# Stores and expert-weight transfers of a fused attention and mixture-of-experts kernel, issued from other queues

## The chip, the cores and the metric

The kernel runs on 1 core of one Trainium2 chip. The metric is the device time of one execution in microseconds (us): the median of three runs. A separate execution is taken under the hardware profiler; every duration of a single instruction below comes from that one.

## What is computed

x is (2, 4096, 512), float32 throughout. For each of the two batches a condition vector gives six rows of shifts, scales and gates. Cut to what matters:

```
h   = layernorm(x) * (1 + ca) + sa
q, k, v = h @ w_qkv.T            # 16 heads of 32; q, k = relu(q), relu(k)
vk  = sum over all tokens of v (padded with ones) times k      # linear attention
x   = x + ga * ((vk @ q) / normaliser @ w_proj.T + b_proj)
h   = layernorm(x) * (1 + cb) + sb
logits = rmsnorm(h) @ router;  two of eight experts per token
x   = x + gb * sum over the two experts of weight * (gelu(h@Wg) * (h@Wv)) @ Wl
```

The sum over all tokens of a batch stands between two passes over that batch: the first makes q, k and the sum, the second needs the sum.

## The kernel before

**Tiling.** A block is 512 tokens of one batch, as four tiles of 128 partitions x 512 features; a batch has eight blocks. Large products go by a seven-product scheme (Strassen's, in Winograd's form) on quarters of the operands, so that both sides need precomputed sums of quarters.

**Stages.** *First passes* (`firsts`, `first`): for each block TensorE makes k and q in fourteen steps (line 717), VectorE scales them out of PSUM (728), ScalarE applies Relu in place (774), then TensorE multiplies x by k into the sum (`pa`, 795). The token-side sums of quarters are made by GpSimd in `turned_sums` (679 to 682): four operations on the transposed block xT that SyncE has loaded (201). In the first batch their target `xs` has one buffer, so line 679 of a block waits until TensorE has done the products of the block before; in TensorE's order the product that needs line 681 is the third of seven, that of 679 the fourth, that of 682 the last. *Second passes* (`seconds`): `attend` loads q tiles back (883), two tiles ahead, normalises, transposes and projects them, adds the residual (952) and stores x to `out` (974); `second_norm` makes h (994, 998; one buffer), stores it to `h_d` (1007), and `route` scatters token slots to `map_d` (1153). *Experts* (`block`, `smalls`): rows of h are gathered by expert, and TensorE runs gate and output products (1512, 1705, 1731); results are added to `out` by indirect transfers from GpSimd. The first pass of batch 1 runs among the second pass of batch 0, and the second pass of batch 1 among the first expert blocks.

**Expert weight sums.** The experts' products need sums of quarters of their weights too. `weight_sums` (584 to 621) makes them in 24 jobs during the first passes of batch 0: load 1 MB of weights into one of two buffers (`wraw`, 598), four GpSimd operations on 128x512 (617), store 1 MB back (618). Two loads are in flight ahead; the load for job n+2 stands behind the store of job n. The expert stage reads the sums after about 860 us. `firsts` takes one job at three points of every block (line 1233).

**What sets the order.** Each engine runs its own instruction stream in order, and a DMA is an instruction in the stream of the engine that issues it: if it has to wait, everything behind it waits. The order inside a stream is chosen at build time by a list scheduler from the order of the program's text and the steps of its generators. In the kernel before, all plain loads and the wraw stores are issued by SyncE (SP in the profile), the stores of q, `out` and h by ScalarE (ACT), and GpSimd (POOL) issues indirect transfers only. Plain transfers of SP and ACT share eight completion semaphores that are taken in turn, so that a transfer can also have to wait until the eighth one before it has landed; those of GpSimd have eight of their own.

Of the kernel before, what the change touches and what calls it, by code (L numbers as in the profile page):

```python
# [17 lines left out]
P = 128  # L18
B, N, C = 2, 4096, 512
# [7 lines left out]
NT = TB // P  # L27
NTOK = B * N
NBLK = N // TB
# [24 lines left out]
def adaln_linear_attention_moe_kernel(  # L54
# [27 lines left out]
    nc = tc.nc  # L82
# [17 lines left out]
        out=upper, in_=ones, compare_op=ALU.is_gt, fill=0.0, base=0,  # L100
# [69 lines left out]
    def place(n, tag, name):  # L170
        return psum["p"].tile([P, 512], FP, tag=f"{tag}{n}", name=name)
# [66 lines left out]
    raw = {}  # L238
# [345 lines left out]
    def weight_sums():  # L584


        jobs = []
        for e in range(E):
            rows = slice(e * P, (e + 1) * P)
            for m in range(2):  # L590
                src = wgate[rows, m * 4 * KH * QN : (m + 1) * 4 * KH * QN]
                r0 = (2 * e + m) * P
                jobs.append((src, wgsum_d[r0 : r0 + P, :], True))
            jobs.append((wlin[rows, :], wlsum_d[rows, :], False))

        def load(n):
            raw = temp(f"wraw_{n}")
            nc.sync.dma_start(out=raw.rearrange("p q n -> p (q n)"), in_=jobs[n][0])
            return raw

        ready = [load(0), load(1)]
        yield
        for n, (_, dst, left) in enumerate(jobs):
            raw = ready.pop(0)
            a, b, c, d = (raw[:, q, :] for q in range(4))
            if left:
                steps = (
                    (c, d, c, ALU.add), (d, a, d, ALU.subtract),
                    (a, c, a, ALU.subtract), (b, b, a, ALU.subtract),
                )  # L610
            else:
                steps = (
                    (a, d, a, ALU.subtract), (d, c, d, ALU.subtract),
                    (c, c, a, ALU.subtract), (b, b, c, ALU.subtract),
                )
            for to, one, two, op in steps:
                nc.gpsimd.tensor_tensor(to, one, two, op)  # L617
            nc.sync.dma_start(out=dst, in_=raw.rearrange("p q n -> p (q n)"))
            if n + 2 < len(jobs):
                ready.append(load(n + 2))  # L620
            yield


# [61 lines left out]
    def first(b, i, acc, ksum):  # L685

        xh, mv = prepared.pop((b, i))
        xs = turned.pop((b, i))
        ks, qs = {}, {}
        out_of = (ks, qs)  # L690
        tile0 = (b * NBLK + i) * NT
        alone = b == 0 and i == 0

        def banks_of(m, c):


            n = c if alone else m
            tags = ("one", "two") if alone or c == 0 else ("two", "one")
            return [place(n, tag, f"p{m}{tag}_{b}_{i}_{c}") for tag in tags]

        def lane(m, c):

            one, two = banks_of(m, c)
            at = E if m else 0
            top, low = slice(0, QN), slice(QN, C)
            for t in (c, c + 2):
                if m:
                    out_of[m][t] = row("qo", f"q_{b}_{i}_{t}", 4, ap)
                else:
                    out_of[m][t] = row("k", f"k_{b}_{i}_{t}", 4, ap)  # L710
            upper_t, lower_t = out_of[m][c], out_of[m][c + 2]

            def product(s, to):
                f = forms[m, s]
                a = at - (AHEAD.get(s, 0) if m else 0)
                for k in range(KH):
                    nc.tensor.matmul(
                        to[:, a : a + f.shape[2]], xs[s][:, k, c * P : (c + 1) * P],
                        f[:, k, :],
                        start=(k == 0 and s in (1, 2, 7)), stop=(k == KH - 1 and s in (2, 4, 3)),  # L720

                        skip_group_check=True,
                    )

            def keep(t, cols, src, new):

                to = out_of[m][t][:, cols]
                nc.vector.scalar_tensor_tensor(
                    to, src[:, at : at + QN], mv[:, t, 1:2],
                    bias[m, b][:, cols] if new else to, ALU.mult, ALU.add,  # L730
                )

            def logits(t, src, c0, new):
                to = xl[:, tile0 + t, 0:E]
                if new:
                    nc.vector.tensor_copy(to, src[:, c0 : c0 + E])
                else:
                    nc.vector.tensor_tensor(to, src[:, c0 : c0 + E], to, ALU.add)

            behind = at + QN  # L740
            for s in ORDER:
                to = two if s in (2, 7, 4) else one
                product(s, to)
                if s == 1:
                    keep(c, top, to, True)
                    if m:
                        logits(c, to, 0, True)
                elif s == 2:
                    keep(c, top, to, False)
                    if m:  # L750
                        logits(c, to, behind, False)
                elif s == 6:
                    keep(c + 2, top, to, True)
                elif s == 7:
                    keep(c + 2, low, to, True)
                elif s == 5:
                    keep(c + 2, low, to, False)
                    if m:
                        logits(c + 2, to, behind, True)
                elif s == 4:  # L760
                    keep(c + 2, top, to, False)
                    if m:
                        logits(c + 2, to, behind, False)
                else:
                    keep(c, low, to, True)
                yield
            for t in (c + 2, c):
                r = out_of[m][t]
                if m == 0:
                    if i == 0 and c == 0 and t == 2:  # L770
                        nc.vector.tensor_scalar(ksum, r, 0.0, None, ALU.max)
                    else:
                        nc.vector.scalar_tensor_tensor(ksum, r, 0.0, ksum, ALU.max, ALU.add)
                nc.scalar.activation(r, r, AF.Relu)  # L774
                if m:
                    r0 = (b * NBLK + i) * P
                    nc.scalar.dma_start(out=q_d[r0 : r0 + P, t * C : (t + 1) * C], in_=r)

        for lanes in (
            ((0, 0), (0, 1)), ((1, 0), (1, 1))  # L780
        ) if alone else (
            ((0, 0), (1, 0)), ((0, 1), (1, 1))
        ):
            going = [lane(*l) for l in lanes]
            for n, s in enumerate(ORDER):
                for g in going:
                    next(g)
                if n == len(ORDER) - 1:
                    for g in going:
                        next(g, None)  # L790
                yield
        for g in range(KC):
            pa = place(g // 2, ("one", "two")[g % 2], f"pa_{b}_{i}_{g}")
            for t in range(NT):
                nc.tensor.matmul(  # L795
                    pa, xh[t][:, g * P : (g + 1) * P], ks[t],
                    start=(t == 0), stop=(t == NT - 1),
                )
            if i == 0:
                nc.vector.tensor_copy(acc[:, g, :], pa)  # L800
            else:
                nc.vector.tensor_tensor(acc[:, g, :], pa, acc[:, g, :], ALU.add)
            yield
        if b + 1 < B and i == NBLK - 1:
            for n in range(2):
                spread_bias(n, b + 1)
# [89 lines left out]
    def attend(b, i, kall, gm):  # L896
# [3 lines left out]
        qs = {}  # L900
# [63 lines left out]
        for step in range(NT + 2):  # L964
            if step < NT:
                weigh(step)
            if 1 <= step <= NT:
                turn(step - 1)
            if step >= 2:
                project(step - 2)  # L970
            if step == NT and i + 1 < NBLK:
                load_xb(b, i + 1)
            if step == NT + 1:
                nc.scalar.dma_start(
                    out=out[r0 : r0 + TB, :].rearrange("(p t) c -> p t c", t=NT), in_=xt
                )
            yield

    def second_norm(b, i):
# [11 lines left out]
        for step in range(NT + 2):  # L991
            if step < NT:
# [10 lines left out]
                nc.scalar.activation(  # L1003
                    sq, h2[:, step, :], AF.Square, accum_out=ssq[:, j : j + 1]
                )
            if step == NT:
                nc.scalar.dma_start(
                    out=h2_d[r0 : r0 + TB, :].rearrange("(p t) c -> p t c", t=NT), in_=h2
                )
                if b + 1 < B and i == NBLK - 1:  # L1010
                    for n in (SB, CB):
                        batch_row(n, b + 1)
# [876 lines left out]
```

## Time and profile before

| what | value |
|---|---|
| median of 3 runs | 2304.97 us (2301.86 to 2310.61) |
| the profiled execution's own time | 2372.11 us |
| its span, first to last instruction | 2370.4 us |
| mean granted TensorE clock | 0.981 |
| HBM read, written | 378.97 MB, 132.55 MB |
| q0, transfers issued by GpSimd | 296.79 MB, 40.1% of the 16 DMA engines' span |
| q1, issued by SP | 164.45 MB, 20.4% |
| q10, issued by ACT | 50.34 MB, 5.5% |

The profiled execution takes 67 us (2.9%) more than the median of the runs. In its rows, L12 is a line of the kernel before; PE is TensorE's matmul, PEld its weight load, DVE is VectorE; a q behind an engine's name (SPq, ACTq) marks an issued DMA, which is not counted as busy time. `out<-in` names the tile written and the tile read; `[6.87 <-ACT k L774]` at the end of a row says that the engine was idle for 6.87 us before it, and what released it.

### The profile page before, as it was taken

How to read it: one execution, taken by the hardware profiler on the slowest of the kernel's cores; microseconds unless marked ns; L12 is line 12 of the kernel's file. 1: busy time of each engine (PE TensorE's matmuls, PEld its weight loads, DVE VectorE, ACT ScalarE, POOL GpSimd, SP SyncE). 2: the span in 40 equal slices, each digit the busy share in tenths (PEclk: the TensorE clock that was granted, in tenths of full speed). 3: DMA queues.
4: the chain of work that ended last, by engine and by line, in shares of the span. 5: the costliest groups of instructions: out<-in, count | busy, mean ns of one | idle time of the engine just before them, and what ended most of it. 6: DMA issues, size and time to landing. Idle time of an engine off the chain costs nothing. (4 is left out here: it accounts for less than half of the span.)

```text
span 2370.4 us, 26081 instructions
## 1 busy us (share of the span) xinstructions
PE 2257.7 (95%) x9456; PEld 1702.1 (72%) x9456; DVE 1523.0 (64%) x3251; ACT 535.0 (23%) x976; POOL 963.2 (41%) x840
## 2 busy tenths in 40 slices
PE   8999989999988999989998889999999999999997
PEld 4576657777766758878887767777777777777775
DVE  4866647786977756767876765555555555555554
ACT  1121212232323302333333411111111111111110
POOL 1266663003223242343535356444444444544432
PEclk9999999999999999999999989999999999999999
DMA  7688886444544444647684557777777777777774
GB/s 271 244 310 324 333 313 230 166 152 138 178 164 110 127 160 166 215 152 239 171 256 150 162 169 241 250 249 247 249 250 250 235 237 248 244 249 256 245 222 89
DMA packets 120189, 513.29 MB, mean 217 GB/s; under 512 B 19365, under 2 KB 22181, under 8 KB 84090
## 3 DMA queue, kind: packets, MB, share of 16 engines
q0 software_dynamic: 64704, 296.79, 40.1%
q1 hardware_dynamic: 41530, 164.45, 20.4%
q10 hardware_dynamic: 13824, 50.34, 5.5%
q8 instruction: 77, 1.26, 0.2%
q14 instruction: 54, 0.44, 0.1%
HBM read 378.97 MB, written 132.55 MB: 216 GB/s over the span
## 5 line engine op out<-in xcount | busy, mean ns | idle before, releaser
L1512 PE MATMUL p_g<-xT,wg 128*128 128x256 f32 x1600 | 373.0, 380 | 0.0
L1512 PEld LDWEIGHTS p_g<-xT,wg 128*128 128x128 f32 x1600 | 303.4, 191 | 45.7 <-issue 5.2
L1512 PE MATMUL p_g<-xS,wg 128*128 128x256 f32 x1200 | 286.6, 381 | 14.9 <-DVE quar_l L1520 7.6
L1512 PEld LDWEIGHTS p_g<-xS,wg 128*128 128x128 f32 x1200 | 227.4, 191 | 51.2 <-issue 8.1
L946 PE MATMUL po<-gm,qT 128*128 128x265 f32 (+1 forms) x1024 | 247.2, 391 | 4.6 <-issue 2.6
L795 PE MATMUL pa<-k,xh 128*128 128x512 f32 x512 | 234.2, 611 | 16.4 <-ACT k L774 16.3
L946 PEld LDWEIGHTS po<-gm,qT 128*128 128x128 f32 x1024 | 194.3, 194 | 40.2 <-issue 5.5
L1488 POOL DMA_INDIRECT out<-y_b,mp x100 | 162.7, 1627 | 129.2 <-DVE y_b L1485 101.2
L1153 POOL DMA_INDIRECT map_d<-pair,slot x128 | 133.5, 1043 | 176.0 <-DVE slot L1150 138.4
L1705 PE MATMUL pgs<-wgs,xTs 128*128 128x512 f32 x464 | 203.9, 592 | 0.0
L1512 PE MATMUL p_l<-wl,aT 128*128 128x256 f32 x800 | 193.7, 380 | 2.6 <-DVE part_l L1520 2.6
L795 PEld LDWEIGHTS pa<-k,xh 128*128 128x128 f32 x512 | 99.0, 196 | 134.4 <-issue 108.1
L617 POOL TENSOR_TENSOR wraw<-wraw 128x512 f32<-128x512 f32 x96 | 135.7, 1417 | 88.9 <-DMA wraw<-in_wgate 36.0
L1705 PEld LDWEIGHTS pgs<-wgs,xTs 128*128 128x128 f32 x464 | 88.2, 190 | 110.5 <-issue 109.5
L1512 PEld LDWEIGHTS p_l<-wl,aT 128*128 128x128 f32 x800 | 148.8, 191 | 23.6 <-DVE part_l L1520 3.0
L1512 PE MATMUL p_l<-wl,aS 128*128 128x256 f32 x600 | 144.0, 383 | 0.6 <-DVE aS L1622 0.6
L679 POOL TENSOR_TENSOR xs<-xT 128x512 f32<-128x512 f32 x16 | 21.3, 1330 | 292.1 <-DMA xT<-in_xturned 173.1
L1520 DVE TENSOR_TENSOR quar_g<-part_g,p_g 128x512 f32<-128x512 f32 x150 | 102.5, 684 | 51.1 <-PE p_g L1512 46.5
L1611 ACT ACTIVATE ge<-quar_g 128x512 f32<-128x512 f32 x100 | 63.0, 630 | 312.2 <-DVE quar_g L1520 300.9
L1512 PEld LDWEIGHTS p_l<-wl,aS 128*128 128x128 f32 x600 | 114.3, 192 | 17.9 <-issue 1.4
L1421 POOL DMA_INDIRECT xg_b<-h_d,mp x100 | 100.9, 1009 | 64.1 <-issue 32.5
L1520 DVE TENSOR_TENSOR part_g<-part_g,p_g 128x512 f32<-128x512 f32 x100 | 68.5, 686 | 83.8 <-PE p_g L1512 78.8
(343 smaller groups left out, 3734.7 us busy)
## 6 DMA issues: line engine op xcount, KB each, us to landing
xT<-in_xturned SPq DMA_DIRECT2D x16, 1024.0 KB
x<-in_x SPq DMA_DIRECT2D x16, 1024.0 KB
q_d<-q ACTq DMA_DIRECT2D x64, 256.0 KB
xb_d<-x SPq DMA_DIRECT2D x16, 1024.0 KB
qi<-q_d SPq DMA_DIRECT2D x64, 256.0 KB
wraw<-in_wgate SPq DMA_DIRECT2D x16, 1024.0 KB
wgsum_d<-wraw SPq DMA_DIRECT2D x16, 1024.0 KB
xb<-xb_d SPq DMA_DIRECT2D x16, 1024.0 KB
```

What stands on the lines that cost most here:

```text
L617: nc.gpsimd.tensor_tensor(to, one, two, op)
L679: nc.gpsimd.tensor_tensor(s7, x00, x10, ALU.subtract)
L795: nc.tensor.matmul(pa, xh[t][:, g * P : (g + 1) * P], ks[t], start=(t == 0), stop=(t == NT - 1),)
L946: nc.tensor.matmul(po[:, C // 2 - EX + c0 : C // 2 - EX + c1], qT[:, g * P : (g + 1) * P], gm[:, g, c0:c1], start=(g == 0), stop=(g == KC ...
L1153: ins = nc.gpsimd.indirect_dma_start(out=map_d, out_offset=IndirectOffsetOnAxis(ap=slot[:, k, t : t + 1], axis=0), in_=pair[:, k, t, :], i ...
L1421: return nc.gpsimd.indirect_dma_start(out=dst, out_offset=None, in_=src, in_offset=IndirectOffsetOnAxis(ap=ids, axis=0))
L1488: ins = nc.gpsimd.indirect_dma_start(out=out[0:N, :] if early else out, out_offset=IndirectOffsetOnAxis(ap=token(mp, t), axis=0), in_=y, i ...
L1512: nc.tensor.matmul(bank[:, c, :], left(s, c, k), rhs[:, k, :], start=(k == 0), stop=(k == KH - 1),)
L1520: nc.vector.tensor_tensor(r, one, two, ALU.add)
L1611: nc.scalar.activation(ge, g, AF.Gelu_apprx_tanh)
L1705: nc.tensor.matmul(p, xT[:, k, :], wg[:, :, quarters[k // KH], k % KH, :], start=(k == 0), stop=(k == KC - 1),)
```

## The change

The 64 stores of q tiles go from ScalarE's stream to SyncE's, and are written later in the text: the tiles of each lane pair together, ahead of the second and of the fourth `pa` product. The 16 stores of x to `out` and the 16 stores of h go from ScalarE's to SyncE's, those of h one generator step later. The 24 loads and 24 stores of the weight sums go from SyncE's to GpSimd's. One load is written ahead of the loop instead of two, and the load of job n+1 ahead of the four operations of job n.

```diff
@@ weight_sums
-            nc.sync.dma_start(out=raw.rearrange("p q n -> p (q n)"), in_=jobs[n][0])
+            nc.gpsimd.dma_start(out=raw.rearrange("p q n -> p (q n)"), in_=jobs[n][0])
             return raw
-        ready = [load(0), load(1)]
+        ready = [load(0)]
         yield
         for n, (_, dst, left) in enumerate(jobs):
+            if n + 1 < len(jobs):
+                ready.append(load(n + 1))
             raw = ready.pop(0)
...
             for to, one, two, op in steps:
                 nc.gpsimd.tensor_tensor(to, one, two, op)
-            nc.sync.dma_start(out=dst, in_=raw.rearrange("p q n -> p (q n)"))
-            if n + 2 < len(jobs):
-                ready.append(load(n + 2))
+            nc.gpsimd.dma_start(out=dst, in_=raw.rearrange("p q n -> p (q n)"))
             yield
@@ first, lane
                 nc.scalar.activation(r, r, AF.Relu)
-                if m:
-                    r0 = (b * NBLK + i) * P
-                    nc.scalar.dma_start(out=q_d[r0 : r0 + P, t * C : (t + 1) * C], in_=r)
@@ first
         for g in range(KC):
+            if g in (1, 3):
+                for t in range(g // 2, NT, 2):
+                    r0 = (b * NBLK + i) * P
+                    nc.sync.dma_start(
+                        out=q_d[r0 : r0 + P, t * C : (t + 1) * C], in_=qs[t]
+                    )
@@ attend
             if step == NT + 1:
-                nc.scalar.dma_start(
+                nc.sync.dma_start(
                     out=out[r0 : r0 + TB, :].rearrange("(p t) c -> p t c", t=NT), in_=xt
                 )
@@ second_norm
-            if step == NT:
-                nc.scalar.dma_start(
+            if step == NT + 1:
+                nc.sync.dma_start(
                     out=h2_d[r0 : r0 + TB, :].rearrange("(p t) c -> p t c", t=NT), in_=h2
                 )
```

In the built program of the changed kernel, GpSimd's stream in the first passes of batch 0 reads, from job 8 on, as a chain of: load of job n+1, store of job n, the four operations of job n+1, load of job n+2, and so on, with the four operations of `turned_sums` spread between them. For blocks 2 to 7 they stand within jobs 2 and 3, 7 and 8, 11 and 12, 15 and 16, 20, and behind job 21.

## The prediction

> **What bounds the kernel now.** I read the page's engine totals first, then the waits, then a table of the first-pass blocks of batch 0, then the timeline where TensorE stood still.
>
> ```profile
> PE 2257.7 (95%) x9456; PEld 1702.1 (72%) x9456; DVE 1523.0 (64%) x3251; ACT 535.0 (23%) x976; POOL 963.2 (41%) x840
> ```
>
> TensorE is busy 95% of the span: 112.7 us is all that any change of queues can give back, and whatever holds TensorE up is added in full. Waits, over the whole span and then from 100 to 400 us:
>
> ```profile
> PE pa L795 <- ACT k L774: 16.3, 4, 8.4
> ...
> POOL wraw L617 <- DMA wraw<-in_wgate: 36.0, 7, 6.8
> POOL wraw L617 <- DMA wraw<-in_wlin: 29.3, 6, 7.4
> ```
>
> Of all that ScalarE does, TensorE waits for Relu of k (16.3 us in 4 waits) and for little else. GpSimd waits 65 us for weights to land, and nobody waits for GpSimd: no row has TensorE behind it in these blocks. How near it is shows in the table by block (bounds from the first product of each) and the timeline.
>
> ```profile
> 265.40:306.30 40.90, 38.89 (x145) 27.11 (x144) 25.80 (x56) 7.93 (x13) 24.71 (x20) 1.00 0.88 335
> 306.30:355.40 49.10, 41.58 (x145) 28.28 (x144) 25.07 (x56) 8.05 (x13) 33.45 (x25) 0.90 0.84 319
> 355.40:395.90 40.50, 38.69 (x146) 27.21 (x145) 28.25 (x64) 8.04 (x13) 17.38 (x13) 1.00 0.79 291
> ```
>
> The columns are the stretch, PE, PEld, DVE, ACT, POOL, granted clock, DMA share, GB/s. A block takes 39.6 us, TensorE works 38.8 of it, GpSimd 25, the DMA engines 77 to 96% over the seven blocks of this table. The middle block took 49.1:
>
> ```profile
> 306.94 1.27 POOL L681 TENSOR_TENSOR xs<-xT 128x512 f32<-128x512 f32 x1
> ...
> 331.90 0.61 ACT L774 ACTIVATE q<-q 128x512 f32<-128x512 f32 x1
> 339.43 0.34 ACTq L777 DMA_DIRECT2D q_d<-q  x1
> 339.81 0.63 ACT L774 ACTIVATE k<-k 128x512 f32<-128x512 f32 x1 [7.29 <-DMA wlsum_d<-wraw]
> ...
> 340.49 7.80 PE L795 MATMUL pa<-k,xh 128*128 128x512 f32 x11 [6.87 <-ACT k L774]
> ```
>
> ScalarE stood at a store of q until a weight-sum transfer had landed; Relu of k stood behind it, TensorE behind that. After the gap 10.2 us ran at half clock (the 0.90 of this stretch: 4.9 us lost). And line 681 ended at 308.2 where TensorE needs it at 309.8 (block start 306.3 plus two products of 1.75): GpSimd had 1.6 us to spare.
>
> **Part 1, 96 stores leave ScalarE.** Their issue is not busy time and ScalarE is at 23%. What it frees is the wait above: 6.9 + 4.9 us, and about 1 us of smaller ones: -13 in this execution. On SyncE 96 x 0.33 us are added and 48 x 0.35 leave, beside a queue that mostly waits: nothing by itself. But SyncE's stream is passed in order: behind a q store that waits for Relu stand the loads of x and xT (needed a block, 40 us, later); behind an h store stands a load of q, needed by the next `attend` step. A step is (694.0 - 638.6) / 6 = 9.2 us. I take 0, with -3 and +30 as ends (the second rival).
>
> **Part 2, 48 transfers of 1 MB enter GpSimd's stream.** Three terms.
>
> Issue: no such transfer is in this trace. The nearest are the indirect loads of 128 rows from the same queue: 0.95 us each, so 46 us of GpSimd in all. Bounds are the 0.33 of SyncE's issues and the 1.6 of the indirect adds (L1488); as both issues of a job lie inside the wait for its load, neither moves the sum while L is over 2 x 1.6.
>
> Landing: for the same 1 MB from SyncE I find issue 276.24, operations released 282.51 (6.3); 358.64 to 363.64 (5.0, DMA share 0.79); most others 6.9 to 7.0. From GpSimd's queue there is
>
> ```profile
> 1405.09 0.30 issue
> 1405.39 3.81 DMA xg_b<-h_d,mp
> 1409.25 0.69 PE px L1579 x2
> ```
>
> 3.8 us for 256 KB; 768 KB more at 291 to 335 GB/s makes 6.2 to 6.5. I take L = 6.0, bounds 4.4 and 7. The lower end is the Trainium skill's (DMA: Bandwidth & Descriptors, "Anatomy of one DMA — SWDGE (gpsimd) path"), which fits a transfer from this queue as 2.0 us plus bytes over 436 GB/s: 4.4. The rows say longer, since other traffic keeps the DMA engines at over 0.79.
>
> Order: in the built program the load of job n+1 is issued right ahead of the operations that use it, in GpSimd's own stream. What was fetched ahead now is waited for: one job is L + 4 x 1.33 = 11.3 us (both issues lie inside L). Between the sums of block 3 and those of block 6 stand 13 jobs, 147 us, while TensorE needs 3 x 39.6 = 119. Stepping through the stream (operation 1.33, issue 0.95, store landing 7.0, load n+2 behind the landing of store n, line 679 behind the last product of the block before), line 681 ends at
>
> | block | ends | needed if TensorE is not held up | late by |
> |---|---|---|---|
> | 3 | 200.9 | 188.8 | 12.1 |
> | 4 | 244.6 | 228.3 | 16.3 |
> | 5 | 292.6 | 267.9 | 24.7 |
> | 6 | 344.1 | 307.5 | 36.6 |
>
> Block 7 finds its sums early, and jobs 22 and 23 are out of the way. So block 8 starts at 106.3 + 7 x 39.5 + 36.8 = 419.7 instead of 395.9. That contains part 1 (no wait at 333): +23.8. Stalls of 4 to 12 us will be followed by half clock as the one of 6.9 was; where GpSimd sets the pace this is hidden, and with 3.5 to 5 us for each stall over 3 us the same stepping gives 424.7: +28.8. I take +27.
>
> The same stepping gives -2 to +2 for L = 4.4, +7 to +12 for 5, +44 to +49 for 7. So the skill's price would make this change free, SyncE's rows make it cost up to 49.
>
> A rule that speaks against the change: "SBUF — State Buffer", "The 'DVE blocks DMA' trap (SWDGE)": descriptors of this queue are written by GpSimd, and VectorE copies in a two-port mode lock it out; its example goes from 0.62 to 3.1 us, which here is L = 8.5 and about +75. VectorE's rows in these blocks are tensor_tensor, scalar_tensor_tensor and statistics, with copies only of 128x8 out of PSUM; the indirect loads of the trace keep 0.95 us beside VectorE at 64%. I take 0 of it.
>
> After block 8 TensorE is the bound again (48 to 60 us busy of every 60, to the end), and it waits there for VectorE, ScalarE and gathers that start later by the same delay, so the delay stays. The profiled execution would go from 2372 to 2399. The median of the runs is 67 us less; nothing in the +27 is tied to the profiler, so I put it on 2305: **2332**.
>
> **The rivals.** *GpSimd keeps up* (0.24). If loads land in 4.4 us or less, its stream is ready when TensorE is, and only the relief of ScalarE is left: at 3.5 us the stepping gives -12, so 2293. For it: the skill's fit, and a DMA load that is spread over a longer time. Against it: no 1 MB load of the trace lands under 5.0. Below 4.4 it is faster, at 4.4 to 5 the same. *SyncE's queue becomes the wait* (0.12). h has one buffer; line 994 of the next block waits, at the head of VectorE, until the store has landed. Before, a store issued at 768.4 was followed by 994 at 780.9: 12.6 us, of which some 5 are the landing. 7.6 us are to spare and the store moves by 9.2. Three such waits cost VectorE 8.0 us before (longest 3.8); eight more at 3.8 are +30 on top: 2362. Against it: in the built order the h operations stand well ahead of the q loads' users, and VectorE is at 64%. *No effect at all* would need both 1 and 2 to cancel, which is the first rival near L = 4.4.
>
> **How the numbers follow.** Within 0.5%, about what a measurement of this kernel can tell from no change, is 2293.4 to 2316.5. GpSimd sets the pace in blocks 3 to 6: 0.64, slower by over 0.5%. The first rival: 0.11 faster, 0.13 the same. The second: 0.10 slower, 0.02 the same. Together 0.11, 0.15, 0.74. The range goes from the first rival's middle, 2299, to L = 7 with part of the second, 2368.
>
> **What the profile after should show.** Waits of TensorE's products on GpSimd's xs (L682 and neighbours of the changed file) of some 37 us, in three or four blocks between 185 and 345 us; wraw operations that wait for their load about 4 to 5 us each, 24 times; block 8's first product near 420; ScalarE free of the 7.3 us wait; half clock in slices 4 to 6; a span from there on unchanged. I am wrong if block 8 starts before 405 (L is small), if its delay is given back in batch 1, or if VectorE's h operations wait for stores.

## The result, and the profile after

The changed kernel takes 2361.64 us (median of 4 runs, 2360.93 to 2363.73) where the kernel before takes 2303.41 (4 runs, 2300.5 to 2310.61): ratio 1.025, interval 1.0224 to 1.0275. It is 58 us slower. The forecast was 2332: the sign and the place were right, and the loss was half of what came.

One caution for reading the two profiles: the kernel before took 2304 us in some sets of runs and 2365 to 2375 in others, for a reason that stays open, and its profiled execution above is of the second kind while that of the changed kernel (2362.15 us, span 2360.4) belongs to a set where it took 2303. So the two spans differ by -10 us although the kernels differ by +58. Of the 112.7 us in which TensorE stood before, some 44 lie in ten stops of 2.4 to 8.4 us behind 560 us, of which the changed kernel's profile has the two near 1380 only. I therefore read *places* in the trace of before, and take times from a kernel of the experiments below, `outh_only`: it differs from the one before by 32 stores, has the ratio 0.9997 to it, and took 2303.32 us in its profile.

Engine totals and waits of the changed kernel, the latter from 60 to 450 us (the last columns are us in total, times, longest):

```profile
PE 2245.0 (95%) x9456; PEld 1704.3 (72%) x9456; DVE 1526.5 (65%) x3251; ACT 534.3 (23%) x975; POOL 980.9 (42%) x888
```

```profile
PE p0one L718 <- POOL xs L682: 53.2, 5, 19.8
PE p1one L718 <- DVE q L729: 5.0, 1, 5.0
```

```profile
POOL wraw L620 <- DMA wraw<-in_wgate: 50.8, 13, 8.5
POOL wraw L620 <- DMA wraw<-in_wlin: 35.5, 7, 7.7
POOL wraw L598 <- DMA wgsum_d<-wraw: 19.4, 4, 8.7
...
POOL wraw L598 <- DMA wlsum_d<-wraw: 6.6, 2, 5.3
```

The engine totals tell nothing: 95% as before. The waits show where the time went. TensorE, which waited for no GpSimd row in these blocks, now waits 53.2 us for line 682 (681 before). GpSimd waits 86 us for loads, where it waited 75 in the same stretch of `outh_only`, and, which is new, 26 us at line 598: it stands at the *issue* of a load until the store that had its buffer has landed. The wait of TensorE for Relu of k is gone.

First-pass blocks of batch 0: blocks 3 to 6 of `outh_only`, then blocks 1 to 6 of the changed kernel (stretch, PE, PEld, DVE, ACT, POOL, granted clock, DMA share, GB/s); the last row of each is all the rest:

```profile
184.40:223.90 39.50, 38.88 (x146) 27.16 (x145) 24.73 (x56) 7.94 (x13) 23.73 (x20) 1.00 0.84 318
223.90:264.20 40.30, 38.68 (x145) 27.15 (x144) 25.24 (x56) 8.05 (x13) 24.43 (x18) 1.00 0.86 325
264.20:305.10 40.90, 38.89 (x145) 27.11 (x144) 25.77 (x56) 7.94 (x13) 24.67 (x20) 1.00 0.88 335
305.10:353.60 48.50, 41.41 (x145) 28.15 (x144) 24.62 (x56) 8.05 (x13) 33.29 (x25) 0.93 0.83 320
...
392.90:2301.60 1908.70, 1872.33 (x8125) 1451.48 (x8123) 1276.71 (x2699) 461.67 (x859) 772.88 (x680) 0.99 0.66 207
```

```profile
105.10:153.60 48.50, 42.08 (x146) 28.86 (x145) 31.26 (x60) 8.05 (x13) 23.21 (x21) 0.89 0.98 369
153.60:194.40 40.80, 38.98 (x145) 27.10 (x144) 26.64 (x56) 8.03 (x13) 22.28 (x22) 1.00 0.91 328
194.40:254.70 60.30, 40.50 (x146) 28.64 (x145) 25.99 (x56) 8.05 (x13) 36.53 (x34) 0.83 0.66 239
254.70:301.40 46.70, 41.34 (x145) 29.26 (x144) 25.89 (x56) 8.03 (x13) 29.11 (x28) 0.93 0.71 258
301.40:353.10 51.70, 41.73 (x146) 29.33 (x145) 26.47 (x56) 8.05 (x13) 32.00 (x28) 0.87 0.70 256
353.10:411.00 57.90, 40.98 (x145) 29.05 (x144) 23.66 (x56) 8.02 (x13) 36.98 (x32) 0.85 0.53 187
...
449.50:2360.40 1910.90, 1872.98 (x8125) 1453.77 (x8123) 1276.05 (x2699) 461.66 (x859) 768.03 (x677) 0.99 0.66 207
```

Block 8 starts at 449.5 in place of 392.9: +56.6. From there to the end it is 1910.9 against 1908.7: +2.2. The whole loss is made before block 8, and is not given back. In blocks 1 and 2 of the changed kernel the DMA engines are busy 0.98 and 0.91 of the time. In blocks 3 to 6, where TensorE stops, their share *falls*, from over 0.8 to 0.53 to 0.71, while GpSimd waits for transfers: there the engines are not full, the transfers are badly placed.

How one stop is made, from GpSimd's and TensorE's rows:

```profile
280.83 0.56 POOL L598 DMA_DIRECT2D wraw<-in_wlin  x1
281.39 0.54 POOL L621 DMA_DIRECT2D wgsum_d<-wraw  x1
289.61 5.29 POOL L620 TENSOR_TENSOR wraw<-wraw 128x512 f32<-128x512 f32 x4 [7.68 <-DMA wraw<-in_wlin]
...
306.82 0.56 POOL L598 DMA_DIRECT2D wraw<-in_wgate  x1
307.39 1.27 POOL L680 TENSOR_TENSOR xs<-xT 128x512 f32<-128x512 f32 x1
308.60 0.57 POOL L621 DMA_DIRECT2D wgsum_d<-wraw  x1
309.18 1.28 POOL L681 TENSOR_TENSOR xT<-xT 128x512 f32<-128x512 f32 x1
312.33 1.26 POOL L620 TENSOR_TENSOR wraw<-wraw 128x512 f32<-128x512 f32 x1 [1.86 <-DMA wraw<-in_wgate]
313.55 1.26 POOL L682 TENSOR_TENSOR xs<-xT 128x512 f32<-128x512 f32 x1
```

```profile
304.07 1.05 PE L718 MATMUL p1two<-q,xT 128*128 128x264 f32 x4
314.86 2.07 PE L718 MATMUL p0one<-k,xs 128*128 128x256 f32 x4 [9.73 <-POOL xs L682]
316.72 1.92 PE L718 MATMUL p1one<-q,xs 128*128 128x256 f32 x4
```

The load of 280.83 has a store issued 0.56 us behind it, and its operations begin 8.78 us after the issue. That of 306.82 stands alone until 308.60, and is there 5.51 us after its issue. Line 682 stands behind both. TensorE stops for 9.73 us, and the products behind the stop run at half clock (2.07, 1.92 us where four such took 1.03; the granted clock is 0.50 from 307.2 to 320.9 us).

### The profile page after: what moved, and what is told of

Its sections match the earlier page's. It is cut to its first block, busy times and chain, and to the rows that moved or that the text cites. A ratio compares the mean times of both kernels' runs of the same rounds, so it can differ in the third digit from the quotient of the medians.

```text
span 2360.4 us, 26038 instructions
## 1 busy us (share of the span) xinstructions
PE 2245.0 (95%) x9456; PEld 1704.3 (72%) x9456; DVE 1526.5 (65%) x3251; ACT 534.3 (23%) x975; POOL 980.9 (42%) x888
## 5 line engine op out<-in xcount | busy, mean ns | idle before, releaser
L951 PE MATMUL po<-gm,qT 128*128 128x265 f32 (+1 forms) x1024 | 239.7, 383 | 0.7 <-ACT qT L943 0.7
L800 PE MATMUL pa<-k,xh 128*128 128x512 f32 x512 | 227.3, 598 | 0.0
L620 POOL TENSOR_TENSOR wraw<-wraw 128x512 f32<-128x512 f32 x96 | 130.6, 1363 | 90.4 <-DMA wraw<-in_wgate 50.8
```

Of the source, the lines that this page charges most:

```text
L800: nc.tensor.matmul(pa, xh[t][:, g * P : (g + 1) * P], ks[t], start=(t == 0), stop=(t == NT - 1),)
L951: nc.tensor.matmul(po[:, C // 2 - EX + c0 : C // 2 - EX + c1], qT[:, g * P : (g + 1) * P], gm[:, g, c0:c1], start=(g == 0), stop=(g == KC ...
```

## The experiments

Ratios are to runs of the kernel before taken alongside, with a 95% interval. "Block 8" is the start of the first pass of batch 1. The letters in the expectations name explanations; two carry the argument. A: the loss is made of landings that are waited for in GpSimd's own stream. M: it is made by the place that the scheduler gives the operations on xs in that stream, counted in weight-sum jobs ahead of them.

**before_again.** No edit: the kernel before in a second profiled execution.

> The kernel before, unchanged, profiled a second time, because its first profiled execution took 67 us more than the median of the runs. If the stop at a store of q near 333 us, the half clock behind it and the eight stops of TensorE between 560 and 1420 us belong to the kernel, they come back and the span is near 2370. If they belong to that one execution, the span is near 2302, the stops after 400 us shrink by some 50 to 65 us in all with the half clock behind them, and block 8 (first pass, batch 1, block 0) starts between 384 and 397: 386 if the stop at 333 is one of them, 396 if it is not.

2374.65 us beside 2368.69 (27 runs of the same kernel alongside). Nine stops of more than 2.4 us behind 400 us are there again, at nearly the same places, so they don't belong to a single execution. The stop near 333 is absent and block 8 starts at 389.3.

**stores_only.** The three edits of the diff in `first`, `attend` and `second_norm` without that in `weight_sums`.

> Only the 96 stores move to SyncE; the weight sums keep SyncE's queue and two loads ahead. Theory A (the loss is made by GpSimd's stream alone): 0 to -12 us against before, ratio 0.995 to 1.000, block 8 at 384 to 397. Rival B (SyncE's stream or the wait of VectorE's h operations on the h store makes part of the loss): +15 to +30 us, ratio 1.007 to 1.013, block 8 as before and the time lost in batch 1.

1.0023 (1.001 to 1.0036), +5 us. VectorE's h operations wait 1.3 us for the h store (9.1 in before_again): rival B is out, and so is my relief of 13 us: these stores cost a little.

**sums_only.** The edit in `weight_sums` without the other three.

> Only the 48 transfers of the weight sums move to GpSimd, one load ahead as in the change; the 96 stores stay on ScalarE. Theory A: GpSimd's stream alone makes the loss, +50 to +70 us, ratio 1.022 to 1.030, block 8 at 440 to 455 and TensorE waiting some 50 us for xs. Rival B: half of the loss at most, +25 to +35, ratio about 1.013. Rival C (the 5.0 us stop at 120 us and the half clock after it, where VectorE's forms stand ahead of a q operation, come from the stores): the same as A, less about 9 us.

1.0244 (1.0218 to 1.0271), block 8 at 450.0. TensorE, from 100 to 450 us:

```profile
PE p0one L718 <- POOL xs L682: 59.4, 5, 16.1
```

The 48 transfers make the whole loss. The stop at 120 us is not there (rival C had expected 9 us less for that), another of 12.6 us at 150 is, for xs, and the loss is the same.

**sync_one.** The changed kernel with the weight transfers on SyncE, one load ahead.

```diff
-            nc.gpsimd.dma_start(out=raw.rearrange("p q n -> p (q n)"), in_=jobs[n][0])
+            nc.sync.dma_start(out=raw.rearrange("p q n -> p (q n)"), in_=jobs[n][0])
...
-            nc.gpsimd.dma_start(out=dst, in_=raw.rearrange("p q n -> p (q n)"))
+            nc.sync.dma_start(out=dst, in_=raw.rearrange("p q n -> p (q n)"))
```

> The changed kernel with the loads and stores of the weight sums given back to SyncE, but one load ahead, as the change writes it. Theory A (it is the queue: in GpSimd's own stream a load can only be issued behind the operations before it): within 12 us of before, ratio 0.995 to 1.005. Rival D (it is the order of the text, one load ahead in place of two): the loss stays, +40 to +60, ratio 1.017 to 1.026.

1.0088 (1.0055 to 1.012), +21 us, between the two forecasts. 10.2 us of it are one stop of TensorE at 407. VectorE's row there:

```profile
416.58 0.48 DVE L729 SCALAR_TENSOR_TENSOR k<-p0one,mv,bias 128x256 f32<-128x256 f32 x1 [10.75 <-DMA bias<-fixed_d]
```

SyncE had stood at a store of sums until 397.9, and issued these rows at 409.6, behind four stores of q. So my rival "SyncE's queue becomes the wait" came true in this mixture. One load ahead on SyncE costs a third of the loss at most.

**q_only** and **outh_only.** The stores in two halves: the q hunks of the diff alone, and the hunks in `attend` and `second_norm` alone.

> Only the 64 stores of q move to SyncE, all else as before. With all 96 stores moved the ratio was 1.0023, where the prediction had -13 us. Theory G (the small loss comes from the first passes, where the q stores' new place makes the scheduler put q products of a block behind the k products of the next): 1.001 to 1.004. Theory H (it comes from h and its single buffer): 0.996 to 1.000, by the relief of ScalarE.

> Only the 32 stores of x to out and of h move to SyncE, those of h a step later; q's stay on ScalarE. Theory G: 0.999 to 1.001. Theory H: 1.002 to 1.006, with VectorE's h operations waiting longer for the h store than the 8 to 9 us of before.

1.0017 (1.0009 to 1.0024) and 0.9997 (0.9986 to 1.0008). Theory G. The stop at the q store is real: outh_only, where q's stores still stand on ScalarE, has it.

```profile
330.27 0.62 ACT L774 ACTIVATE q<-q 128x512 f32<-128x512 f32 x1
337.80 0.34 ACTq L777 DMA_DIRECT2D q_d<-q  x1
338.19 0.63 ACT L774 ACTIVATE k<-k 128x512 f32<-128x512 f32 x1 [7.30 <-DMA wlsum_d<-wraw]
```

Its block 6 takes 48.5 us in place of 39.4: 9.1 us. In q_only it is gone, but blocks 2 and 3 take 95.4 us together (143.8 to 239.2) against 78.7 in outh_only: the scheduler, with the stores elsewhere, puts q products of block 2 behind k products of block 3, and TensorE waits in many small gaps for VectorE's k and q. What the move gave was given back where I had not looked.

**two_ops.** The changed kernel with two of the four operations of each job.

```diff
-            for to, one, two, op in steps:
+            for to, one, two, op in steps[:2]:
```

> The changed kernel with only the first two of the four operations of each weight-sum job: the sums in memory are then not those of the reference, and 48 of 1.27 us are taken from GpSimd's stream. Theory A (landing and operations add up in one stream, job by job): the stepping with loads of 5.4 us alone and 7.9 with a store behind them, and stores of 8.5 to 9.5, gives block 8 some 33 us earlier than in the change, so a ratio to before of 1.007 to 1.014. Rival F (the DMA rate sets the pace of the jobs, and the operations only fill the wait): under 12 us earlier, ratio 1.020 or more.

1.0098 (1.0078 to 1.0117), block 8 at 414.4 where it was 449.5: 35 us earlier for 33 stepped. TensorE waits 23.7 us for xs in place of 53.2. Landing and operations add up, job by job; rival F is out.

**four_bufs.** The changed kernel with four buffers and loads ahead.

```diff
-            raw = temp(f"wraw_{n}")
+            raw = temp(f"wraw_{n}", None if n % 4 < 2 else 1)
...
-        ready = [load(0)]
+        ready = [load(0), load(1)]
...
-            if n + 1 < len(jobs):
-                ready.append(load(n + 1))
+            if n + 2 < len(jobs):
+                ready.append(load(n + 2))
```

> The changed kernel with its queues, but the raw weights turn over four buffers (the two of before and two that lie idle in these passes) and the load of job n+2 is written ahead of the operations of job n, so that neither a landing of a load nor one of a store is waited for at the head of GpSimd's stream. Theory A (the loss is made of landings waited for in GpSimd's own stream): nearly all of it goes, ratio to before 0.998 to 1.006 (what the moved stores cost by themselves, +5, and 4 us), block 8 near 390 to 398, the waits of GpSimd for wraw under 20 us in place of 86. Rival E (the issues on GpSimd, or GpSimd's descriptors held up by VectorE, make transfers from this queue slow in themselves, so that the queue does not keep up whatever the number of buffers): at least half the loss stays, ratio 1.012 to 1.025.

1.0139 (1.0117 to 1.0161), +32: theory A had +4, and it falls into rival E's range. The waits of TensorE for xs did go, from 53.2 to 7.5 us, and GpSimd's for loads from 86 to 10; its waits for stores to land did not (28 us at line 598, 26 in the change), so the run is a test of the waits for loads alone. Block 8 still starts at 424.7. Eight us are lost before block 1 (113.9 for 105.6), 23.5 in blocks 1 to 7. A part of these lies between VectorE and GpSimd, as rows of both show:

```profile
271.90 5.19 DVE L774 SCALAR_TENSOR_TENSOR ksum<-k,ksum 128x512 f32<-128x512 f32 x1
277.02 0.47 DVE L729 SCALAR_TENSOR_TENSOR k<-p0two,mv,bias 128x256 f32<-128x256 f32 x1
277.42 5.15 DVE L774 SCALAR_TENSOR_TENSOR ksum<-k,ksum 128x512 f32<-128x512 f32 x1
```

```profile
271.61 4.93 POOL L620 TENSOR_TENSOR wraw<-wraw 128x512 f32<-128x512 f32 x4
276.49 0.58 POOL L621 DMA_DIRECT2D wgsum_d<-wraw  x1
277.09 4.92 POOL L620 TENSOR_TENSOR wraw<-wraw 128x512 f32<-128x512 f32 x4
```

The sum of k takes 0.67 us in the mean where no GpSimd operation lies beside it (16 of 32 in these passes) and 1.95 where one does: six of these 16 are no longer than alone, two of over 5 us are as long as a row of four GpSimd operations. VectorE does nothing else in that time, and TensorE stands behind it (4.41 us up to 283.09, until line 737 of VectorE is through). With its waits for loads taken away GpSimd works in bursts, and some of the bursts stop VectorE.

**before_noksum** and **four_noksum.** The sum of k left out of both.

```diff
-                    else:
-                        nc.vector.scalar_tensor_tensor(ksum, r, 0.0, ksum, ALU.max, ALU.add)
```

> The kernel before with VectorE's running sum of k over the tiles left out (62 operations on two 128x512 operands in SBUF; the normaliser of the attention then has the sum of one tile only). It is the measure for the next run. TensorE is the bound here, so little: ratio 0.995 to 1.000, whichever theory is right.

> The changed kernel with four weight buffers (+32 us, where +4 was expected, although TensorE hardly waits for xs any more) and VectorE's running sum of k left out, as in the run before it. Theory J (what is left of the loss is VectorE held up by GpSimd: the sum of k took up to 5.19 us in place of 0.66 beside a row of GpSimd operations, and Relu of k and TensorE stand behind it): the difference to the kernel before with the same left out falls to +8 to +18 us (8 of it are lost before block 1, and the residual addition with its two operands stays). Rival E (transfers from GpSimd's queue slow in themselves): it stays at +28 to +34.

1.0268 and 1.037. Without the sum tokens go to other experts, and both kernels get a stop of 22 us near 2290; only their difference counts. It is 22.3 us (2389.14 - 2366.88) where it was 32, and at block 8 it is 16.9 (408.8 against 391.9) where it was 31.8 (424.7 against 392.9). The forecast of theory J, 8 to 18, holds at block 8 and not at the end. And of the 14.9 us that block 8 gains, 7.2 are gained ahead of block 1 (110.0 against 108.9 there, where it was 113.9 against 105.6). From block 1 to block 8 the loss goes from 23.5 to 15.8: the sum of k is about a third of what four_bufs loses there, and the other two thirds stay open (the wait for stores at line 598, and the residual addition, 2.3 us on two operands, are candidates that were not tried).

**split_ls** and **sums_back.** Loads on GpSimd and stores on SyncE; and the kernel before with its 24 sum stores on GpSimd.

```diff
-            nc.sync.dma_start(out=dst, in_=raw.rearrange("p q n -> p (q n)"))
+            nc.gpsimd.dma_start(out=dst, in_=raw.rearrange("p q n -> p (q n)"))
```

> The changed kernel with the loads of the weights on GpSimd's queue and the stores of their sums on SyncE's. In the built order two loads of the pair stand together and then eight operations. Theory A: a load that isn't waited for behind a store costs 5.4 us, a pair some 7 to 8 to the second landing, so two jobs take 8 + 10.2 us plus the wait for SyncE's store, 18 to 20 in place of 2 x 13; the loss is +10 to +35 us, ratio 1.004 to 1.015. Rival K (any wait for a landing in GpSimd's stream costs the same, wherever the store is issued): +50 to +65, ratio 1.022 to 1.028.

> The kernel before with only the 24 stores of the weight sums moved to GpSimd, behind the operations that make them; loads stay on SyncE two ahead, the other stores on ScalarE. Nothing on GpSimd waits for a landing then, and the stores no longer share completion semaphores with ScalarE's q stores, so the stop of Relu of k behind a q store near 332 us (6.5 us and half clock) should go. Theory A: ratio 0.995 to 0.999, faster than both kernels by 2 to 10 us. Rival L (any transfer from GpSimd's queue costs, by its issue and by VectorE's and GpSimd's shared access): 1.003 to 1.010.

1.023 (1.0209 to 1.0251), which is in rival K's range, and 1.0252 (1.0236 to 1.0269), which is outside both forecasts. Both are against theory A as I had it. In sums_back nothing on GpSimd waits for a landing that did not wait before, and it should have been the better kernel. TensorE waits 38.9 us for xs in it, and 20.6 for Relu of k behind a q store, the stop that was to go. Its stream shows another cause. The operations of line 681 for blocks 3, 4 and 5 stand behind 8.75, 14.25 and 20.5 jobs, in the kernel before behind 7, 11 and 14. In split_ls they stand behind 8.5, 13 and 18.25, so that run can't tell landings from places. In the changed kernel it is 8.25, 12 and 16.25. Hence theory M, the place, and six more kernels.

**before_late_xs, before_new_order, before_old_order.** The kernel before, SyncE's queue and all, with xs pinned behind chosen numbers of jobs. The edit of the first; in the others the numbers differ:

```diff
-                if n == 0 and done == 2 * SEVEN:
-                    for _ in range(4):
-                        next(wsums, None)
-                elif n and done in (0, SEVEN, 2 * SEVEN):
+                for _ in range({(1, 0): 2, (1, SEVEN): 1, (1, 2 * SEVEN): 1, (2, 0): 2, (2, SEVEN): 2, (2, 2 * SEVEN): 2, (3, 0): 2, (3, SEVEN): 2, (3, 2 * SEVEN): 1, (4, 0): 2, (4, SEVEN): 2, (4, 2 * SEVEN): 2, (5, 0): 1, (5, SEVEN): 1, (5, 2 * SEVEN): 1, (6, 0): 1, (7, SEVEN): 3}.get((n, done), 0)):
                     next(wsums, None)
...
-            for to, one, two, op in steps:
-                nc.gpsimd.tensor_tensor(to, one, two, op)
+            for k, (to, one, two, op) in enumerate(steps):
+                ins = nc.gpsimd.tensor_tensor(to, one, two, op)
+                if not k:
+                    tc.keep_in_program_order(ins)
...
-        nc.gpsimd.tensor_tensor(s7, x00, x10, ALU.subtract)
+        ins = nc.gpsimd.tensor_tensor(s7, x00, x10, ALU.subtract)
+        if not b and i > 1:
+            tc.keep_in_program_order(ins)
```

> The kernel before, all transfers on its queues, but xs of blocks 2 to 7 pinned behind 3, 9, 14, 20, 23 and 24 weight-sum jobs (before: 2, 7, 11, 14, 18.25, 23). Theory M (place): GpSimd ends a job every 10.6 us, so xs of block 4 comes 3 jobs later, at 258 in place of 226 (needed at 228), that of block 5 at 325 in place of 262 (needed at 268): +45 to +60 us, ratio 1.019 to 1.026. Theory A (landings in GpSimd's stream): nothing on GpSimd waits for more than before, so +0 to +8, ratio under 1.004.

> The kernel before, all transfers on its queues, with xs pinned near the places of the changed kernel: behind 2, 8, 12, 16, 20 and 23 jobs. Theory M: xs of block 5 at 283 where it is needed at 268, that of block 6 at 327 where it is needed at 307: +15 to +30 us, ratio 1.006 to 1.013. Theory A: +0 to +5, ratio under 1.002.

> The control: the kernel before, all its queues, with xs pinned behind 2, 7, 11, 14, 18 and 23 jobs, where the scheduler had them anyway (18 for 18.25). If the pins cost something by themselves (the first weight load is issued later, and GpSimd's first job waited 27.6 us for it), the ratio is 1.003 to 1.008 with a stop of 8 to 14 us near 190 us, and the places of the changed kernel cost next to nothing on SyncE's queue. If pins are free, the ratio is 0.999 to 1.001, and the 12 us of before_new_order are the price of the places.

1.0259 (1.0205 to 1.0312): the loss of sums_back, in theory M's range, without one transfer on GpSimd. 1.0051 (1.0032 to 1.007) with the places of the changed kernel, less than M and more than A had, and 1.0054 (1.0036 to 1.0072) for the control with the places of before. TensorE in before_late_xs:

```profile
PE p0two L721 <- POOL xs L681: 58.5, 4, 21.7
```

So a late place alone can cost about 2% (1.0259 less the pins' 0.5%), nearly as much as the whole change, but the places of the *changed* kernel cost nothing while the transfers are SyncE's: 1.0051 and 1.0054 are the same, the price of the pins.

**sums_back_old** and **after_old_order.** The same pins at the places of before, with the 24 stores, and with all of the change, on GpSimd.

> The kernel before with the 24 stores of the weight sums on GpSimd (ratio 1.025 where the scheduler placed xs), but with xs pinned behind 2, 7, 11, 14, 18 and 23 jobs, as they stood before. Theory M: the loss goes, ratio 0.997 to 1.004. Rival L (any transfer issued on GpSimd costs that much): 1.018 to 1.026.

> The changed kernel with all its queues, but with xs pinned behind 2, 7, 11, 14, 18 and 23 jobs, as before the change. In the stream that this makes, the load of job n+2 stands right behind the store of job n, whose landing it waits for. Theory M: the loss falls from 58 to +0 to +25 us, ratio 1.000 to 1.011. Theory A: the stepping with loads of 5.4 and 7.9 and stores of 7 to 8.5 gives block 8 at 439 to 472, so +45 to +80, ratio 1.020 to 1.035.

1.0115 (1.008 to 1.0149), between the forecasts: less the pins' 0.54%, three quarters of sums_back's loss was the place. What is left shows as 18.1 us of TensorE's waits for Relu of k. 1.0212 (1.0155 to 1.0268): with the places of before the change still loses 50 us, 37 without the pins (that the price of the pins can simply be taken off is an assumption). Block 8 starts at 436.6, where theory A had 439 to 472, and at 407.6 in the control. In its stream GpSimd waits 92.5 us for stores to land (62.9 and 29.6, at line 598) and 5.7 for loads, which the pins put further ahead of their use. Theory A for the change, with stores in the place of loads; theory M for most of sums_back.

**after_spread.** The change with two jobs a block over both batches, by the same dictionary with other numbers, the same pins, and one more on the loads.

```diff
-            nc.gpsimd.dma_start(out=raw.rearrange("p q n -> p (q n)"), in_=jobs[n][0])
+            ins = nc.gpsimd.dma_start(out=raw.rearrange("p q n -> p (q n)"), in_=jobs[n][0])
+            tc.keep_in_program_order(ins)
```

> The changed kernel with all its queues, but with two jobs a block over the first passes of both batches (xs of blocks 2 to 7 behind 1, 3, 5, 7, 9 and 11 jobs, the rest in batch 1; the loads are pinned in order too). A job still waits for two landings in GpSimd's stream, 12 to 14 us. Theory A (the landings cost only because 3 to 5 jobs a block don't fit): 2 x 13 + 5 us fit into the 39.5 us of a block, so ratio 0.996 to 1.004 and no waits of TensorE for xs in batch 0. Rival M (what costs is transfers among the other work of GpSimd, wherever): 1.008 to 1.02, with the loss in batch 1, where GpSimd scatters token slots too.

1.0198 (1.0173 to 1.0222). In batch 0:

```profile
229.40:268.20 38.80, 38.52 (x145) 27.28 (x144) 23.74 (x56) 8.03 (x13) 17.64 (x16) 1.00 0.58 217
```

```profile
221.37 0.57 POOL L598 DMA_DIRECT2D wraw<-in_wgate  x1
221.96 5.32 POOL L621 TENSOR_TENSOR wraw<-wraw 128x512 f32<-128x512 f32 x4
...
231.98 0.53 POOL L598 DMA_DIRECT2D wraw<-in_wgate  x1 [3.83 <-DMA wlsum_d<-wraw]
232.52 5.37 POOL L621 TENSOR_TENSOR wraw<-wraw 128x512 f32<-128x512 f32 x4
```

From block 2 on no block loses a microsecond: TensorE waits for no xs, and block 8 starts at 384.2, the earliest of all kernels. But the waits are not those that the expectation names. The pins keep each load one job ahead, and from block 3 on the operations behind a load, which are those of the job before, start at once: no load is waited for. Of the landings only that of a store is, 3.8 us once a block, and GpSimd stands idle for 16 us more in each. So transfers from GpSimd's queue cost nothing where the loads are fetched ahead and two jobs go to a block; that two waited landings a job would fit too was not tried.

The other half of the jobs meets GpSimd's own work in batch 1. There TensorE waits 34.8 us for xs (24.2 and 10.6, from 384 to 900 us), and GpSimd 45 us for stores of sums to land. Theory A's forecast for batch 0 came, rival M's in batch 1. No version tried is faster than the kernel before.

## Why the prediction was half right

*GpSimd's stream sets the pace of blocks 3 to 6, and line 681 is the late one.* Right: 53.2 us of waits for it where "some 37" were named, block 8 at 449.5 and not before 405, nothing given back in batch 1 (+2.2 us from there on).

*The landing, L = 6.0.* This is the term that failed: over the 24 loads it is 7.5 us in the mean, from the issue to the landing or the first use. Three groups stand in the trace. The first eight, up to 195 us, where the DMA engines are busy 0.91 to 0.98 of the time, took 5.4 to 13.5, 9.2 in the mean. Of the 16 loads from 208 us on, 8 have a store issued 0.55 us behind them and land after 6.7 to 9.6 us, 7.9 in the mean; the 8 that stand alone, or with a store at least 1.8 us behind, after 5.0 to 5.6, 5.4 in the mean. (sums_only has the same two groups: 7.0 to 8.6 and 5.1 to 5.8.) My estimate was for a load among other traffic, and not for a load with a store at its heels, though the table of the order that I stepped through had them side by side. The store need not be GpSimd's: in split_ls SyncE issues it, 0.1 us behind the load, and nine such loads are first used after 7.4 to 9.6 us. A store whose landing a load waits for took 7.4 to 10.9 us in four of six cases, and I had 7.0 for all.

What this cost can be read at line 682, in GpSimd's stream. For block 3 it ended at 217.9 where I had stepped to 200.9, 17.0 late; for block 6 at 373.7 where I had 344.1, so 12.6 more in the 13 jobs between. Together that is 29.6 us, and block 8 is 29.8 later than stepped (449.5 for 419.7). As an estimate, with 5.4, 7.9 and 8.5 to 9.5 for such stores in the same stepping block 8 comes at 434 to 443; the long landings of the first eight loads are not in that. That the loss is a sum over jobs, and not a rate of the DMA engines, two_ops shows by its 35 us.

*Issue 0.95 us.* Measured 0.53 to 0.57 (the first 0.77), and without weight, as the text said.

*Half clock.* The text read 10.2 us at half clock "after the gap", 4.9 us lost. The gap lasted from 333.6 to 340.5, and the clock was already halved in it (the last three columns are granted clock, DMA share, GB/s):

```profile
333.60:336.00 2.40, 0.03 (x1) 0.00 (x0) 0.00 (x0) 0.00 (x0) 2.32 (x3) 0.99 0.07 27
336.00:340.40 4.40, 0.00 (x0) 0.00 (x0) 0.00 (x0) 0.59 (x2) 4.17 (x4) 0.50 0.96 400
340.40:346.20 5.80, 5.71 (x7) 2.52 (x8) 0.18 (x1) 0.56 (x2) 0.40 (x2) 0.50 1.00 330
```

Only the 5.7 us behind the stop cost anything, 2.9, and PE in that block is 2.8 us over its neighbours (41.58 for 38.89 and 38.69). In the change half clock reaches 4.0 to 6.0 us past the end of each of the four stops from 198 us on. Behind the first three a longer stop for xs follows than the half clock costs, so it is hidden there, as the text said; the last adds 2.6, where the sum had 3.

*Part 1, -13.* Wrong, and in the sign: +5. The stop is worth 9.1 us, and it goes, but the new place of the q stores makes the scheduler reorder blocks 2 and 3 for more than that. I had costed the moved stores in SyncE's stream and never compared TensorE's own order. In the whole change this hardly weighs: sums_only, without these stores, loses as much.

*What was not in the sum, and did not need to be.* Block 1 takes 48.5 us for 39.6. Here a wait stands ahead of a q operation on VectorE:

```profile
120.10 3.31 DVE L364 TENSOR_TENSOR latersums<-later 128x512 f32<-128x512 f32 x2 [2.15 <-DMA forms_d<-later]
123.33 1.75 DVE L364 TENSOR_TENSOR latersums<-later,latersums 128x512 f32<-128x512 f32 x1
125.00 0.47 DVE L729 SCALAR_TENSOR_TENSOR q<-p1one,mv,bias 128x256 f32<-128x256 f32 x1
```

The built order of the changed kernel has these forms some 30 rows further down VectorE's stream than before. TensorE stops 5.0 us for the q operation, and half clock follows. Neither part of the change does it alone (39.6 and 39.5 us in stores_only and sums_only). But these 8.9 us are not a part of the loss: sums_only does without them, waits 12.6 us for xs in block 2 instead, and reaches block 8 at 450.0, the change at 449.5. GpSimd's stream sets the pace already there.

*The rivals.* GpSimd does not keep up: the first rival needed loads of 4.4 us, and the shortest of the 24 took 5.0. SyncE's queue is no wait in the changed kernel: its h operations wait 4.4 us for h's store, once, where before it was 8.0 in three waits. (The text's "994 at 780.9" is line 952 in the trace; 994 follows at 783.4, so 10.0 us were to spare there and not 7.6.) The Trainium skill's price for such a transfer ("DMA: Bandwidth & Descriptors", the anatomy of a transfer from this queue), 4.4 us, was below each landing measured here; the lock-out of this queue by VectorE ("SBUF — State Buffer", "The 'DVE blocks DMA' trap (SWDGE)") could be taken at 0 in this kernel, as issues stay at 0.53 to 0.57 and lone loads at 5.0 to 5.6 beside VectorE at 41 to 55% of its time; no run here has large VectorE copies beside them.

## What to carry to other kernels

A transfer that moves into a computing engine's own stream can turn a landing that was fetched ahead into a wait at the head of that stream; after_spread, with its loads kept one job ahead, shows that it need not. Cost it by the job (landing, operations, and the landing that its buffer needs), see whether the jobs between two deadlines still fit, and time a load together with the store that will be issued beside it, and in the busiest stretch as well as in a quiet one. And compare the built order of *every* engine first, also of those that the diff does not touch: deadline operations placed two to six jobs later cost about 2% here, nearly as much as the whole change, and no diff shows it.

## What was not expected of the hardware

A load and a store of 1 MB issued 0.55 us apart are no faster together than one behind the other. The load lands after 7.9 us where one alone takes 5.4. Of the eight stores at a load's heels the trace has the landing of five, so that both of the pair have landed 9.1 to 12.0 us after the load's issue. Three stores clear of loads (issued at 201.6, 415.1 and 431.3) took 4.1, 4.5 and 7.5, which with 5.4 for the load makes 9.5 to 12.9 in a row: the pair shows no clear gain, and whoever waits for the load waits 2.5 us longer. And a VectorE operation on two operands in SBUF, 0.67 us alone, took up to 5.19 beside four GpSimd operations in a row. "SBUF — State Buffer" of the Trainium skill ("Who interferes with whom") has it that such an operation and a GpSimd operation that reads SBUF exclude each other, the second blocked until the first is through. Here, in four_bufs, VectorE was held twice not for one of GpSimd's operations of 1.23 us but for four, which that page does not have.
